# Two edits to a hand-ordered graph kernel: the order of its four long neighbour lists, and ScalarE's queue in the order of the plan

## The chip, the core and the metric

The kernel runs on one core of a Trainium2 chip. Its engines are TensorE (PE in the profile, with its weight loads as PEld), VectorE (DVE), ScalarE (ACT), GpSimd (POOL) and SyncE (SP), which here only issues DMAs. The metric is the device time of one execution in microseconds; the median over several executions is given.

## What is computed

The input is 16 graphs (`b`) of 1024 nodes with 64 channels, a dense weighted adjacency matrix per graph (mean degree of a few, a few nodes with dozens of neighbours) and a node mask that is all ones. Two layers follow each other:

```python
# layer 0
h = relu(layernorm(x))
x = x + (adj / max(adj.sum(2), 1)) @ h
# layer 1
h = relu(layernorm(x))
# nb[i]: neighbours of i without i.  A node with more than 10 of them
# drops every ceil(m/2)-th one; a pair dropped by either end is gone.
adj_d = dilate(adj, mask)
agg = 0.25*q(0.25) + 0.5*q(0.5) + 0.25*q(0.75)   # per channel, over h of the
                                                 # neighbours left and the node itself,
                                                 # quantiles interpolated between two values
y = relu((h + agg) @ W1 + b1) @ W2 + b2
x = x + y * mask
```

The quantiles need the neighbours' values in sorted order, for each of 64 channels. That sorting, on lists of very different length, is what most of the kernel is about.

## The kernel before

**Two stages.** In the first, the batch stage (0 to about 895 us in the trace), the 16 graphs go through one after the other. Each has eight tiles of 128 adjacency rows. ScalarE takes the sign of a tile (`sg<-at`), VectorE multiplies it with column keys and takes the largest eight keys of each of four segments (`rec<-sg`): these are the neighbour numbers. TensorE transposes the same tile (`pt<-ident,at`), ScalarE copies it out of PSUM (`att<-pt`), and TensorE multiplies it with h (`ps_small<-att,h`). The layer norms are on ScalarE and VectorE. Each node's record is scattered by GpSimd to a DRAM table (`srt<-row`) in order of degree, within groups of four graphs, and its normalised channels are written to a table `tab` per group.

**Jobs.** When a group of four graphs is complete, its nodes are worked off as jobs of `T` times 128 nodes with lists of equal length `n`, longest first. A job has the same parts always (class `Job`, L831): GpSimd gathers the neighbours' rows, one indirect DMA per list position (`places<-tab,idx`); VectorE opens the job (`rem`, `gone`, `ok`, `valid`, `q`, `wu`); ScalarE adds a huge number to the places that are gone (`places<-places,gone`); VectorE runs a sorting network of min and max operations between `places` and `other`; VectorE makes the weights (`w`) and ScalarE or VectorE the weighted values (`prod<-places,w`); TensorE adds these up (`pt<-ident,prod`) and runs the two small matrix products, with ScalarE copies between (`ot`, `hid`); VectorE adds the residual (`y`), and GpSimd scatters the rows to the output (`out_dram<-y`).

**Long lists.** The eight nodes of highest degree in each graph make the first long list, the next eight the second, and so on: four lists of 128 nodes with up to 88, 31, 24 and 20 neighbours (`LONG`, L43; `long_lists`, L1239). They gather from `whole`, a table of all graphs, so they can only run after the last graph. For each list, GpSimd fetches the 128 full adjacency rows (`lat`), VectorE picks the neighbours out of them (`lkey`, `lfound`, `lkeys`) down to indices (`lidx`), and a job follows, whose tiles carry an l (`lplaces`, `lgone`, `lw`). The 88 list has a gather buffer of its own (`lplaces0`); the other three share two (`lplaces`). All four share one second sorting buffer, `long_other` (L945): a list's network can start only after TensorE has read the products of the list before it out of that buffer. In a long list ScalarE writes the weighted values in place, into `lplaces` and `long_other`. The second stage, from about 895 us, holds the jobs that are left of the third group, all of the last group's, and the four long lists.

**What sets the order.** `Plan` (L234) records every instruction through a wrapper (hence the one line L228 in all rows). The work is cut into streams that yield an engine and an earliest time at each point; `Plan.run` (L323) always takes the stream that can begin first by the plan's own clocks, which `note` (L271) advances with a time per operation. An instruction is emitted when its stream is taken. The engines named in `manual_schedule` (L365) execute in this order of emission; the queues of the others are ordered by the framework's scheduler. In the kernel before, VectorE and GpSimd are named. ScalarE's, TensorE's and SyncE's queues are the scheduler's, and ScalarE's departs from the order of emission at 251 points of its queue. The order is static in either case.

Ranks break ties in the plan: `-600 + l` is a long job's gather rank and `100 * NG + l` its sorting rank, where `l` numbers the lists.

Of the kernel before, what the change touches and what calls it, by code (L numbers as in the profile page):

```python
# [39 lines left out]
LONG = (88, 31, 24, 20)  # L40
# [179 lines left out]
class Timed:  # L220


    def __init__(self, plan, name, engine):
        self._plan, self._name, self._engine = plan, name, engine
# [9 lines left out]
class Plan:  # L234
# [4 lines left out]
    def __init__(self, nc):  # L239
        names = {"vector": "DVE", "scalar": "ACT", "tensor": "PE", "gpsimd": "POOL", "sync": "SP"}  # L240
        self.nc = SimpleNamespace(
            **{attr: Timed(self, name, getattr(nc, attr)) for attr, name in names.items()}
        )
        self.clock = dict.fromkeys([*names.values(), "DMA"], 0.0)
        self.ready, self.used, self.users = {}, {}, {}
        self.slots, self.streams = {}, []
        self.last = self.own = None
        self.parts = set()

    def tile(self, pool, shape, dtype, name, bufs, users=0):  # L250

        res = pool.tile(shape, dtype, name=name, bufs=bufs)
        self.slots.setdefault(name, []).append(res.tensor.name)
        self.users[res.tensor.name] = users
        return res
# [12 lines left out]
    def at(self, *tiles):  # L268
        return max(self.ready.get(t.tensor.name, INF) for t in tiles)

    def note(self, engine, op, args, kwargs):  # L271
        if self.own is not None:
            self.clock[engine] = max(self.clock[engine], self.own)
        out = kwargs["out"] if "out" in kwargs else args[0]
        rest = [*args[0 if "out" in kwargs else 1:], *(v for k, v in kwargs.items() if k != "out")]
        rest = [getattr(v, "ap", v) if type(v).__name__.startswith("Indirect") else v for v in rest]
        rest = [v for v in rest if isinstance(v, bass.AP)]
        size = max(math.prod(v.shape[1:]) for v in (out, *rest[:2]))
        start = max(
            self.clock[engine],  # L280
            *(self.ready.get(v.tensor.name, 0.0) for v in rest if self.own is None),
            self.used.get(out.tensor.name, 0.0) if self.own is None else 0.0,
        )
        after = 0.15
        apart = engine == "SP" and out.tensor.name in self.parts
        if apart:
            start = max(self.clock[engine], *(self.ready[v.tensor.name] for v in rest))
        if engine == "DVE":
            half = op == "tensor_tensor" and all(v.dtype == HF for v in (out, *rest))
            time = 0.04 if op == "memset" else 0.07 + size * (0.57e-3 if half else 1.04e-3)  # L290
        elif engine == "ACT":
            pointers = sum(isinstance(kwargs.get(k), bass.AP) for k in ("bias", "scale"))
            time = 0.06 + size * 0.86e-3 + 0.11 * pointers + 0.09 * ("accum_out" in kwargs)
        elif engine == "PE":
            time = 0.1 + math.prod(out.shape[1:]) * 0.88e-3
            if op == "matmul" and rest[0].dtype == F32:
                time *= 2
        elif engine == "POOL":
            time, after = (1.27, 2.2) if op == "indirect_dma_start" else (0.15, 0.1)
            self.last = None  # L300
        else:
            start = max(start, self.clock["DMA"])
            busy = math.prod(out.shape) * 4 / 165e3

            time, after = 0.05, 2.2 + busy * (1 if 4 * out.shape[-1] >= 512 else 2)
            self.clock["DMA"] = start + busy
        self.clock[engine] = end = start + time
        if not apart:
            self.ready[out.tensor.name] = end + after
        for v in rest:  # L310
            self.used[v.tensor.name] = max(self.used.get(v.tensor.name, 0.0), end + after)
        if "accum_out" in kwargs:
            self.ready[kwargs["accum_out"].tensor.name] = end + after
        return start
# [21 lines left out]
@with_exitstack  # L336
def kernel(
    ctx: ExitStack,
    tc: tile.TileContext,
    x: bass.AP,  # L340
    adj: bass.AP,
    nodemask: bass.AP,
    w1: bass.AP,
    b1: bass.AP,
    w2: bass.AP,
    b2: bass.AP,
    out: bass.AP,
):

    nc = tc.nc
    B = x.shape[0]  # L360

    flags = ctx.enter_context(tc.tile_pool(name="flags", bufs=1))
    go = flags.tile([P, 1], I32, name="go")

    with tc.manual_schedule(engines={mybir.EngineType.DVE, mybir.EngineType.Pool}):  # L365
        list_path(tc, x, adj, nodemask, w1, b1, w2, b2, out, go)
    taken = nc.values_load(go[0:1, 0:1], min_val=0, max_val=1)
    with tc.If(taken > 0):
        with tc.For_i(0, B, 1) as b:
            dense_path(tc, b, x, adj, nodemask, w1, b1, w2, b2, out)  # L370
# [3 lines left out]
def list_path(ctx, tc, x, adj, nodemask, w1, b1, w2, b2, out, go):  # L374
# [7 lines left out]
    NG = len(GROUPS)  # L382
# [101 lines left out]
    whole = dram.tile([B * TS, W], F32, name="whole")  # L484
# [11 lines left out]
    plan = Plan(nc)  # L496
    plan.parts.update(tab.tensor.name for tab in tabs)
    nc = plan.nc
    new, free, room, at = plan.tile, plan.release, plan.room, plan.at
# [739 lines left out]
    def long_lists(pool):  # L1239
# [1 line left out]
        yield "DVE", always  # L1241
        rev = new(pool, [P, N], HF, "rev", 1)
        nc.vector.tensor_scalar(rev, col_f, -1.0, float(N), op0=OP.mult, op1=OP.add)
        for l, K in enumerate(LONG):
            n = K + 1
            yield "SP", always
            S = new(pool, [P, 1, RW], F32, "lS", 4)
# [62 lines left out]
            for e in range(2):  # L1310
# [7 lines left out]
            yield "DVE", lambda: 0.0 if progress["groups"] == NG else INF  # L1318
            job = Job(
                pool, n, 1, keys, idx.unsqueeze(1), node, mask, nodes_i, whole, S, NG,  # L1320
                *(("lplaces", 2) if l else ("lplaces0", 1)), -600 + l, begin=at(whole),
            )
            plan.add(job.run(), 100 * NG + l)

    progress = {"batches": 0, "begun": 0, "groups": 0, "ahead": 0, "jobs": [0] * (NG + 1)}
    for g in range(NG - 1):
# [1 line left out]
    with tc.tile_pool(name="lay0", bufs=2) as pool:  # L1328

        for stream, first in (  # L1330
            (endings, 0), (channels, 1), (products, 2), (transposes, 4), (listing, 5),
            (beginnings, 6), (loads, 7), (signs, -15),
        ):
            now = [0]
            plan.add(stream(pool, now), lambda first=first, now=now: 10 * now[0] + first)
        plan.run(lambda: progress["batches"] == B)
    with tc.tile_pool(name="long", bufs=1) as pool:

        plan.add(group(NG - 1, pool, "last_"), -2000)
        plan.add(long_lists(pool), -1500)  # L1340
        plan.run()
# [292 lines left out]
```

## Time and profile before

| what | before |
|---|---|
| median of 3 executions | 1513.86 us (1511.95 to 1516.6) |
| the profiled execution, whole | 1512.82 us |
| its span, first to last instruction | 1511.0 us |
| VectorE busy, 0 to 900 us | 81% |
| GpSimd busy, 900 to 1300 us | 75% |
| indirect DMAs issued by GpSimd after 900 us | 407 |
| one gather on GpSimd: busy, and start to start | 0.94 us, 1.25 us |
| first and last gather of the 88 list | 953.8 us, 1093.9 us |
| its opening, its weights (`lrem`, `lw` on VectorE) | 1096.5 us, 1346.8 us |
| networks of the 31, 24 and 20 lists begin | 1394.4, 1436.0, 1470.5 us |
| last scatter to the output begins | 1502.1 us |

A row of the groups reads: line, engine, operation, the tile written and those read, shape, number of instructions; then busy time and mean duration; then the time the engine idled just before, and what ended it. A row of the waits reads: who waited, for whom, total in us, how many times, the longest.

### The profile page before, as it was taken

How to read it: one execution, taken by the hardware profiler on the slowest of the kernel's cores; microseconds unless marked ns; L12 is line 12 of the kernel's file. 1: busy time of each engine (PE TensorE's matmuls, PEld its weight loads, DVE VectorE, ACT ScalarE, POOL GpSimd, SP SyncE). 2: the span in 40 equal slices, each digit the busy share in tenths (PEclk: the TensorE clock that was granted, in tenths of full speed). 3: DMA queues.
4: the chain of work that ended last, by engine and by line, in shares of the span. 5: the costliest groups of instructions: out<-in, count | busy, mean ns of one | idle time of the engine just before them, and what ended most of it. 6: DMA issues, size and time to landing. Idle time of an engine off the chain costs nothing. (4 is left out here: it accounts for less than half of the span.)

```text
span 1511.0 us, 15983 instructions
## 1 busy us (share of the span) xinstructions
PE 738.8 (49%) x3192; PEld 464.7 (31%) x3192; DVE 1191.3 (79%) x4104; ACT 816.4 (54%) x2789; POOL 957.2 (63%) x1154
## 2 busy tenths in 40 slices
PE   4778777327877556567667620024000123228542
PEld 2434334214544233343444320012000122216432
DVE  6777798997899779859869869893059999986875
ACT  7989878557879457757975520201050223148341
POOL 0122227777678757757777787667777777765083
PEclk8889888658888777869688755555555565558765
DMA  5445665424355253355341242111111111211010
GB/s 177 150 142 168 163 210 160 123 73 114 101 162 152 59 174 94 99 126 161 94 140 31 60 101 68 50 37 28 30 26 23 28 28 40 44 33 22 2 25 13
DMA packets 135718, 133.36 MB, mean 88 GB/s; under 512 B 100756, under 2 KB 103444, under 8 KB 135492
## 3 DMA queue, kind: packets, MB, share of 16 engines
q1 hardware_dynamic: 102876, 90.79, 20.8%
q0 software_dynamic: 32736, 41.47, 11.2%
q14 instruction: 78, 0.64, 0.1%
q8 instruction: 28, 0.46, 0.1%
HBM read 112.90 MB, written 23.61 MB: 90 GB/s over the span
## 5 line engine op out<-in xcount | busy, mean ns | idle before, releaser
L228 POOL DMA_INDIRECT places<-tab,idx x372 | 370.2, 995 | 131.7 <-issue 101.8
L228 PE MATMUL pt<-ident,prod 128*128 128x128 f32 (+1 forms) x736 | 160.2, 377 | 517.8 <-DVE prod L228 241.2
L228 PEld LDWEIGHTS pt<-ident,prod 128*128 128x128 f32 (+1 forms) x736 | 129.3, 256 | 550.4 <-ACT prod L228 412.4
L228 PE MATMUL ps_small<-att,h 128*65 128x512 f32 x512 | 254.7, 644 | 27.3 <-ACT h L228 10.5
L228 POOL DMA_INDIRECT srt<-row,to x128 | 125.9, 984 | 165.8 <-ACT row L228 144.0
L228 PE MATMUL pt<-ident,at 128*128 128x128 f32 x1024 | 176.7, 320 | 96.0 <-ACT att L228 71.1
L228 POOL DMA_INDIRECT lplaces<-whole,lidx x163 | 167.2, 1026 | 55.6 <-issue 48.5
L228 DVE MAX8 rec<-sg 128x8 f16<-128x256 f16 x512 | 180.1, 414 | 4.4
L228 PEld LDWEIGHTS pt<-ident,at 128*128 128x128 f32 x1024 | 136.9, 164 | 143.5 <-ACT att L228 93.8
L228 ACT ACTIVATE sg<-at 128x1024 f16<-128x1024 f32 x128 | 134.8, 1054 | 75.0 <-DMA at<-in_adj_dram 65.7
L228 ACT COPY att<-pt 128x512 f32<-128x512 f32 x256 | 141.9, 582 | 20.7 <-PE pt L228 18.8
L228 POOL DMA_INDIRECT places<-tab,last_idx x124 | 123.8, 998 | 41.3 <-issue 35.0
L228 PEld LDWEIGHTS ps_small<-att,h 128*65 128x65 f32 x512 | 74.7, 151 | 161.9 <-issue 123.2
L228 ACT ACTIVATE places<-places,gone 128x64 f32<-128x64 f32 x496 | 123.5, 335 | 0.5
L228 ACT ACTIVATE prod<-places,w 128x64 f32<-128x64 f32 x213 | 54.1, 336 | 120.5 <-DVE w L228 120.5
L228 POOL DMA_INDIRECT out_dram<-y,nodes_i x93 | 91.8, 987 | 22.6 <-issue 15.1
L228 DVE TENSOR_TENSOR sg<-sg,keyed 128x1024 f16<-128x1024 f16 x128 | 87.2, 681 | 23.7 <-ACT sg L228 23.7
L228 ACT ACTIVATE gone<-gone 128x15 f32<-128x15 f32 (+9 forms) x40 | 8.2, 206 | 169.2 <-DVE ok L228 169.0
L228 DVE TENSOR_TENSOR long_other<-lplaces 128x512 f32<-128x512 f32 (+5 forms) x124 | 64.1, 555 | 29.1 <-ACT lplaces L228 28.9
L228 DVE TENSOR_TENSOR other<-places,other 128x64 f32<-128x64 f32 (+6 forms) x204 | 69.6, 341 | 5.9
L228 PE MATMUL ps_small<-ot,w_sb 128*128 128x128 f32 (+3 forms) x112 | 47.6, 513 | 44.2 <-DVE y L228 31.2
L228 DVE TENSOR_TENSOR places<-places,other 128x64 f32<-128x64 f32 (+2 forms) x208 | 62.3, 309 | 4.9
(231 smaller groups left out, 1670.8 us busy)
## 6 DMA issues: line engine op xcount, KB each, us to landing
at<-in_adj_dram SPq DMA_DIRECT2D x128, 512.0 KB
places<-tab,idx POOLq DMA_INDIRECT x372, 2.5
whole<-tab SPq DMA_DIRECT2D x4, 1057.0 KB
tab<-row SPq DMA_DIRECT2D x16, 264.0 KB
xt<-in_x_dram SPq DMA_DIRECT2D x16, 256.0 KB
lplaces<-whole,lidx POOLq DMA_INDIRECT x163, 2.4
srt<-row,to POOLq DMA_INDIRECT x128, 2.7
places<-tab,last_idx POOLq DMA_INDIRECT x124, 2.4
```

The source lines that it names most:

```text
L228: ins = getattr(self._engine, op)(*args, **kwargs)
```

## The change

Three things are edited. ScalarE joins the engines whose queue keeps the order of emission. The long lists are run in the order 31, 24, 88, 20, with ranks that follow this order; which rows a list holds, its buffers and its capacities stay with the list. And the plan's clock counts a TensorE instruction as 1.5 times as long from the end of the batch stage on.

```diff
@@ class Plan, __init__
         self.parts = set()
+        self.pace = 1.0
@@ class Plan, note, TensorE
             time = 0.1 + math.prod(out.shape[1:]) * 0.88e-3
             if op == "matmul" and rest[0].dtype == F32:
                 time *= 2
+            time *= self.pace
@@ tile_gnn_kernel
-    with tc.manual_schedule(engines={mybir.EngineType.DVE, mybir.EngineType.Pool}):
+    with tc.manual_schedule(engines={mybir.EngineType.DVE, mybir.EngineType.Pool, mybir.EngineType.Activation}):
@@ long_lists
-        for l, K in enumerate(LONG):
+        for nth, l in enumerate((1, 2, 0, 3)):
+            K = LONG[l]
@@ long_lists
-                *(("lplaces", 2) if l else ("lplaces0", 1)), -600 + l, begin=at(whole),
+                *(("lplaces", 2) if l else ("lplaces0", 1)), -600 + nth, begin=at(whole),
             )
-            plan.add(job.run(), 100 * NG + l)
+            plan.add(job.run(), 100 * NG + nth)
@@ list_path, after the batch stage
         plan.run(lambda: progress["batches"] == B)
+    plan.pace = 1.5
     with tc.tile_pool(name="long", bufs=1) as pool:
```

No instruction's kind or shape changes but for a few of ScalarE's and VectorE's products, which the plan shares between the two by its clocks (2405 instructions on ScalarE before, 2431 after; 4025 and 4023 on VectorE; 1154 and 1152 on GpSimd; 296 on SyncE in both). VectorE's and GpSimd's queues are the same as before up to the first list's `lkey` operations, 918.9 us in the trace before; ScalarE's, TensorE's and SyncE's differ from the start.

## The prediction

> **What bounds the kernel now.** I read the page first, then the engines' waits, then the timeline of the last 600 us by engine, then the chain that ended last.
>
> ```profile
> span 1511.0 us, 15983 instructions
> PE 738.8 (49%) x3192; PEld 464.7 (31%) x3192; DVE 1191.3 (79%) x4104; ACT 816.4 (54%) x2789; POOL 957.2 (63%) x1154
> DVE  6777798997899779859869869893059999986875
> ACT  7989878557879457757975520201050223148341
> POOL 0122227777678757757777787667777777765083
> DVE lrem L228 <- DMA lplaces<-whole,lidx: 50.1, 2, 48.9
> DVE y L228 <- PE ps_small L228: 28.1, 4, 14.1
> DVE sg L228 <- ACT sg L228: 23.7, 15, 8.7
> DVE other L228 <- ACT places L228: 14.2, 7, 4.8
> ...
> 1096.53 0.34 DVE L228 TENSOR_TENSOR lrem<-lplaces,lS 128x176 f32<-128x176 f32 x1 [48.89 <-DMA lplaces<-whole,lidx]
> 1378.07 0.57 DVE L228 TENSOR_TENSOR other<-places 128x384 f32<-128x384 f32 x1 [11.20 <-ACT places L228]
> 1394.38 1.22 DVE L228 TENSOR_TENSOR long_other<-lplaces 128x512 f32<-128x512 f32 x2
> 1425.18 0.20 DVE lw L228
> 1425.40 0.35 ACT long_other L228
> 1491.27 3.93 ACT L228 ACTIVATE lplaces<-lplaces,lw 128x64 f32<-128x64 f32 x16 [18.76 <-DVE lw L228]
> 1502.09 0.96 POOL L228 DMA_INDIRECT out_dram<-y,lnodes_i  x1 [1.73 <-DVE bad L1346]
> ```
>
> VectorE is the bound: busy in nearly every slice but those of the digits 3 and 0 (about 1020 to 1096 us), where it waits 14.1 us for a `y` and 48.9 us for the 88 list's gathers. ScalarE is at 8 to 9 tenths only in the first 200 us. From 900 us GpSimd gathers without a pause, 1.25 us apart, to 1382 us. The end is a chain of VectorE, ScalarE and TensorE through the lists 31, 24 and 20, one after the other, because all share `long_other`.
>
> **What the Trainium skill says.** PSUM — Partial Sum Buffer, Engine vs sequencer instructions: "ScalarE/VectorE/GpSimdE queues are strict FIFO." So the order of a queue is a cost by itself: the trace agrees, ScalarE sat 51.7 us before `lgone` until 1097.47. DMA: Bandwidth & Descriptors, Anatomy of one DMA, gives about 2 us fixed per DMA; here a gather lands 2.4 us after its issue. TensorE: Matmul & The Clock Gate, What's actually happening: an idle array runs at half clock; the page shows PEclk 5 from 900 to 1340 us.
>
> **Part 1, ScalarE's queue.** It adds and removes nothing; it takes 251 departures out of the queue (the order of instructions shows none left, so the edit does what it says). Up to the end of the batch stage the kinds that move most are the 128 `row<-rec` (36.1 us in all), 16 `row<-row_f` and 26 `prod<-S`: fillers that ran up to 170 us early and that nobody but a late scatter waits for. Without them, `att<-pt` goes back 7 places in the mean and the work that VectorE waits for (places, prod, norms) forward 3 to 4. VectorE's waits for ScalarE in this stage are 23.7 (sg) + 14.2 (places) + 17.5 (ln_v, two rows) = 55.4 us: the most that could be gained. What could be lost: behind a ScalarE instruction that waits stand `att` copies, then TensorE's two `pt` buffers, then the `at` buffers and SyncE's loads. In the places where an instruction's producer ended later in the trace before than something now behind it, the exposure of the real work is 3 to 13 us at some forty places, on an engine with 30% slack from 200 us on; in the first 200 us ScalarE idles 24 us, which fillers used. SyncE's and TensorE's queues are re-ordered with it, by the scheduler. Bounds: -35 to +20 us; I take 0, since VectorE's own order is unchanged and the swaps are a few places.
>
> **Part 2, the lists, up to the 88 list's opening.** The order of instructions gives GpSimd from 943 us: 31 + 24 + 88 gathers, 1 of list 20, 2 `lat`, 4 `places`, 6 scatters = 156 x 1.25 = 195 us, plus waits for indices. VectorE builds a list's indices in about 20 us (957.1 to 977.0 for 31; 34 for 88), and GpSimd's next `lat` needs the build before it: estimated from these lengths 4.6 us for list 88's `lat` (indices of list 24 ready at 965, GpSimd free at 960.6), 9.3 us for list 20's (ready at 1007, free at 997.5) and 3.5 us for list 31's `y`, which stands in GpSimd's queue among the 88 gathers. SyncE's four loads per list (`lS`, 891 to 901 us) change places among themselves only, before anything needs them. Sum: last gather issued 943 + 195 + 17 - 1 = 1154, opening at about 1156 instead of 1096.5. VectorE meanwhile does more: before 180 us from 916.3, of which 63 idle, so 117 us of work; now also the networks 31 (1394.4 to 1425.0: 30.6) and 24 (1436.0 to 1461.1: 25.1), 173 us in 240. Idle 67 instead of 63: **the wait isn't removed, the 88 list just comes 60 us later with 56 us more done.**
>
> **Part 3, from there to the 88 list's weights.** Before: 1096.5 to 1346.8 = 250.3 us, with 17 us at its start when ScalarE marks 88 places (21.1 us). Now the jobs are further ahead: VectorE did 28.6 us of job work between 1346.8 and 1394.4 (47.6 less waits of 5, 11, 2 and 1); of that kind only 11.7 us are left after `lw` in the new order. So 17 us move ahead of it: 1156 + 250 + 17 = 1423. GpSimd's gathers for these jobs are all in by then (264 us of its queue after 1156, scatters that wait included, ends before VectorE needs them), so it isn't the limit.
>
> **Part 4, the handover of `long_other`.** Before, `lw` at 1346.8, ScalarE's 67 products of the 88 list among job work until 1379.7, TensorE's sums until 1392, next network at 1394.4: 47.6 us, which VectorE filled with 28.6 us of jobs. VectorE's network 20 needs two things: list 20's marks by ScalarE, and TensorE done with `long_other`. Now `lw` at 1423; in ScalarE's queue between there and list 20's marks stand 67 products of list 88, 31 of two jobs with their two copies, 17 marks of the last two jobs, and 6 small ones, 123 at 0.245 us (24 took 5.82 us), and five of 0.6 us (`ot`, `hid`): 33 us, 1457; 20 marks 5 us; TensorE's last 58 products stand behind a `hid` at 1460 and take 13 to 16 us (before: 122 records in 13.5 us). Network 20 begins at 1474 (50 us after `lw`), with 12 us of cover. It takes 20.4 us as before (1470.5 to 1490.9): `lw` of list 20 at 1494.5.
>
> **Part 5, the end.** Before, 20 us from that `lw` (1490.9) to the end, one scatter after the last `y`. Now ScalarE's `ot` copies for two jobs stand behind list 20's 16 products (3.9 us), their sums behind 17 matmuls of list 20 in TensorE's queue (6 us), so `y` of the 88 list comes about 14 us after `lw`, and 13 scatters follow one another from there: 13 x 1.27 = 16.5. Last scatter begins at lw + 29, and 8.9 us follow it (1502.1 to 1511.0): 37 us. Span 1494.5 + 37 = 1531.5.
>
> **Part 6, pace.** It moves no instruction by itself in the batch stage (set after it); what it does to the order is in the counts above.
>
> Sum: span +20.5 us; the profiled execution is 1.8 us longer than its span and 1.0 below the median shown. Forecast 1512.82 + 20.5 = **1533 us**, 1.3% above the median.
>
> **Rivals.**
> A (faster): ScalarE in VectorE's order ends VectorE's waits. For: its rows of waits, 55.4 us in the batch stage, and 11.2 us at 1378 behind the 88 list's products. Against: ScalarE's departures were mostly fillers. At two thirds of 55.4, -37: 1496. It decides from 24 us on.
> B (faster): the handover is hidden better: TensorE adds up as ScalarE writes, as for list 31 (products 1425.7 to 1431.5, sums to 1434.2), network 20 at 1460 and the end 12 us shorter: 1533 - 26 = 1507. Against: 58 of 67 sums stand behind the late `hid`.
> C (no effect): old and new idle match and the scatters at the end overlap: 1514.
> D (slower still): ScalarE, ahead of VectorE, blocks `att` copies and starves the loads: +20 in the batch stage, 1553. For: SyncE waited 323.8 us for TensorE to free `at`. Against: four signs are kept ahead.
>
> **How the numbers follow.** Main case 0.48 (own range 1518 to 1546), A 0.19, B 0.08, C 0.10, D 0.15. Faster by over 0.3% (about what a measurement of this kernel can tell from no change) 0.27, within 0.10, slower 0.63. Range 1498 to 1552: half of A and of D are left out.
>
> **What would show it.** Right: `lrem` of 88 places near 1156 with a wait of some 30 us before it; `lw` of 67 near 1423; a VectorE gap of about 35 us before network 20; a row of scatters after the last `y`. Part 1 shows in the time of `last_recs` work (896 us before). Wrong: that time moved by over 15 us, no gap before network 20, or the 88 list's opening before 1140.

## The result, and the profile after

| | before | after |
|---|---|---|
| median | 1512.9 us (1508.1 to 1516.6, 4 runs) | 1593.0 us (1592.7 to 1601.1, 4 runs) |
| span of the profiled execution | 1511.0 us | 1590.6 us |
| first stage: start to the first work on `last_recs` | 901.4 us | 971.5 us |
| second stage: from there to the end | 609.6 us | 619.1 us |

The change makes the kernel slower by 5.3% (ratio 1.0532, 95% interval 1.0506 to 1.0558). The forecast, 1533 us, had the direction and missed the size. Of the 79.6 us of span, 70.1 are lost before the first long list is touched, and 9.5 after. (From here on a stage is measured from the first `last_keys<-last_recs` on VectorE. The expectations of e1 to e4 count from VectorE's first instruction on `last_recs`, which comes 5 us earlier: 896 us before, 966 after.)

The first fence is from the page of the changed kernel: the span, the engines' busy times, and the slices of VectorE, ScalarE and GpSimd.

```profile
span 1590.6 us, 15958 instructions
PE 789.8 (50%) x3192; PEld 495.9 (31%) x3192; DVE 1193.0 (75%) x4102; ACT 826.0 (52%) x2815; POOL 960.3 (60%) x1152
...
DVE  7666698996687778778749878799750699999851
ACT  7788877656676736574876450114310423221651
POOL 0122227777557763776776487767777877377614
```

VectorE has the work it had (1193.0 us, before 1191.3), but where the slices of the first stage had eights and nines there are sixes, sevens and eights. Nothing was added: the same work waits more. The table of waits of the changed kernel (who waited, for whom; total us, times, longest) says for what:

```profile
DVE sg L228 <- ACT sg L228: 81.0, 40, 8.7
DVE lrem L228 <- DMA lplaces<-whole,lidx: 45.0, 2, 44.4
DVE long_other L228 <- ACT lplaces L228: 37.0, 9, 12.0
DVE y L228 <- PE ps_small L228: 32.1, 6, 11.8
DVE deg L228 <- PE ps_small L228: 30.6, 8, 7.4
...
ACT sg L228 <- DMA at<-in_adj_dram: 94.5, 37, 14.6
...
PE pt L228 <- ACT att L228: 162.2, 59, 8.9
...
SPq L228 <- PE pt L228: 390.5, 110, 15.6
```

Before, VectorE's rows were 23.7 us for `sg` by ScalarE and 50.1 for the 88 list's gathers, and the last three were these:

```profile
ACT sg L228 <- DMA at<-in_adj_dram: 65.7, 27, 24.5
...
PE pt L228 <- ACT att L228: 74.4, 45, 7.4
...
SPq L228 <- PE pt L228: 323.8, 102, 15.8
```

So the 88 list's wait, which the new list order moves, is nearly all still there. What grew is a chain through four engines: TensorE waits 88 us more for ScalarE's `att` copies, SyncE 67 us more for TensorE, ScalarE 29 us more for loads, VectorE 57 us more for signs.

The rows don't add up to the loss, because other waits of TensorE got shorter: in the first stage it waited 17 us for the jobs' products (`prod`) instead of 102. Taken whole, the same 2432 matmul records of TensorE's first stage were busy for 615.0 us instead of 588.8, and TensorE stood idle for 356.5 us instead of 312.7. So 44 of the 70 us are more standing still, and 26 are the same work taking longer.

One stretch of the changed kernel's timeline shows how this goes (start and duration in us, engine, operation, and in brackets the idle time before it and what ended it):

```profile
555.06 1.05 ACT L228 COPY att<-pt 128x512 f32<-128x512 f32 x2
...
555.68 1.97 PE L228 MATMUL pt<-ident,at 128*128 128x128 f32 x8 [0.22 <-ACT att L228]
...
565.45 0.37 SPq L228 DMA_DIRECT2D y<-srt  x1
...
565.92 0.41 SPq L228 DMA_DIRECT2D at<-in_adj_dram  x1
...
570.73 1.06 ACT L228 ACTIVATE sg<-at 128x1024 f16<-128x1024 f32 x1 [14.62 <-DMA at<-in_adj_dram]
...
571.78 0.46 ACT L228 ACTIVATE hid<-ps_small,b_sb 128x256 f32<-128x256 f32 x1
...
572.14 1.06 ACT L228 COPY att<-pt 128x512 f32<-128x512 f32 x2
...
572.29 0.79 PE L228 MATMUL ps_small<-b_sb,ones_f 1*128 1x128 f32 x2 [14.64 <-ACT hid L228]
```

TensorE finished eight transposes (both `pt` buffers) at 557.7. Their two copies could have run then. They stand in ScalarE's queue behind an `sg` whose load SyncE issued only at 565.9, and ScalarE stands still for 14.6 us in front of it. TensorE stands still just as long, for the `hid` behind the same `sg`. The load itself was late here for a reason outside this chain: its buffer had been free since 556.8, when TensorE's last transpose out of it ended, but in SyncE's queue it stood behind a job's load (`y<-srt`), which the profile shows waiting for GpSimd's scatters to the output, 11.7 us. So the stretch shows what a late load does to the copies, not that the copies made this load late. Such hold-ups of SyncE are not what grew: over the stage a buffer lay free for 0.9 us in the mean before its next load was issued, and for 0.6 us in the changed kernel.

Of all time in which ScalarE stood still while a finished `pt` waited for its copy, 153 us fell to an `sg` in the changed kernel, 26 us before (worked out from the trace: gaps of over 0.3 us between the end of the fourth transpose and the start of its copy, by the instruction after the gap).

Two of the five sets of runs below (e5, x4, x5, x6 and z2, z3) fell into spells in which the kernel before itself took 1978 and 1956 us, so their times are given only as ratios to it, and since x4, x5 and x6 gave other ratios when they were run again (as y4, y5 and y6), these ratios settle little.

### The profile page after: what moved, and what is told of

The parts are those of the page before. It is cut to its first block, busy times and chain, and to the rows that moved or that the text cites. A ratio compares the mean times of both kernels' runs of the same rounds, so it can differ in the third digit from the quotient of the medians.

```text
span 1590.6 us, 15958 instructions
## 1 busy us (share of the span) xinstructions
PE 789.8 (50%) x3192; PEld 495.9 (31%) x3192; DVE 1193.0 (75%) x4102; ACT 826.0 (52%) x2815; POOL 960.3 (60%) x1152
## 5 line engine op out<-in xcount | busy, mean ns | idle before, releaser
L228 POOL DMA_INDIRECT places<-tab,idx x372 | 374.5, 1007 | 162.9 <-issue 102.7
L228 PE MATMUL ps_small<-att,h 128*65 128x512 f32 x512 | 270.3, 677 | 17.0 <-DVE row L228 7.0
L228 PE MATMUL pt<-ident,at 128*128 128x128 f32 x1024 | 190.1, 340 | 162.2 <-ACT att L228 139.4
L228 PEld LDWEIGHTS pt<-ident,at 128*128 128x128 f32 x1024 | 147.9, 174 | 214.9 <-ACT att L228 165.4
L228 POOL DMA_INDIRECT lplaces<-whole,lidx x163 | 162.7, 998 | 49.7 <-issue 48.1
L228 POOL DMA_INDIRECT places<-tab,last_idx x124 | 127.5, 1029 | 57.2 <-issue 35.3
L228 PEld LDWEIGHTS ps_small<-att,h 128*65 128x65 f32 x512 | 78.6, 159 | 159.2 <-issue 133.3
L228 ACT ACTIVATE prod<-places,w 128x64 f32<-128x64 f32 x239 | 60.3, 335 | 93.4 <-DVE w L228 93.3
L228 DVE TENSOR_TENSOR long_other<-lplaces 128x512 f32<-128x512 f32 (+6 forms) x124 | 64.0, 555 | 37.2 <-ACT lplaces L228 37.0
L228 PE MATMUL ps_small<-ot,w_sb 128*128 128x128 f32 (+3 forms) x112 | 51.7, 553 | 48.4 <-ACT ot L228 46.3
L228 ACT COPY ot<-pt 128x128 f32<-128x128 f32 (+3 forms) x56 | 21.9, 392 | 95.4 <-PE pt L228 95.2
```

The lines of the kernel that those rows point to most:

```text
L228: ins = getattr(self._engine, op)(*args, **kwargs)
```

## The experiments

The theory H: the loss is ScalarE's queue in the first stage. An `att` copy that stands in line keeps a `pt` buffer, TensorE keeps the `at` buffer, SyncE's next load starts later. The rivals: the lists' edit carries the loss (L); TensorE's and SyncE's queues do, which the scheduler re-orders when ScalarE's is fixed (S); ScalarE merely stands idle behind late operands (W); the plan's TensorE clock is at fault (K).

**1. The change taken apart.** Four kernels, each with a part of the change.

e1_act: the kernel before with

```diff
-    with tc.manual_schedule(engines={mybir.EngineType.DVE, mybir.EngineType.Pool}):
+    with tc.manual_schedule(engines={mybir.EngineType.DVE, mybir.EngineType.Pool, mybir.EngineType.Activation}):
```

> ScalarE's queue in the order of the plan, alone; lists in the old order, no pace. Theory H (the loss sits in ScalarE's queue in the batch stage: att copies, which the scheduler let pass other work, wait in line, TensorE's two pt buffers and SyncE's loads follow): last_recs work at 966 us as in the changed kernel, not 896, and then the old second stage of about 595 us: 1580 us (1565 to 1600). Rival L (the lists' edit carries the loss, through TensorE's and SyncE's queues, which the scheduler orders over the whole kernel): 1513 to 1545 us.

e2_lists: the changed kernel with that line as before.

> The lists' order and the pace, without ScalarE. H: last_recs work at 896 us within 5, then a second stage of 604 to 615 us as in the changed kernel or as my prediction's parts 2 to 5 have it: 1523 us (1510 to 1535). L: last_recs work late by tens of us, 1550 or more.

e3_act_first: the kernel before, its schedule cut in two where the batch stage ends, ScalarE named in the first part only. The edit at the seam:

```diff
         plan.run(lambda: progress["batches"] == B)
+    manual.__exit__(None, None, None)
+    manual = tc.manual_schedule(engines={mybir.EngineType.DVE, mybir.EngineType.Pool})
+    manual.__enter__()
```

> ScalarE in the order of the plan in the batch stage only, lists and pace as before. H: all of the loss of this stage, last_recs work at 966 us, then 595 us: 1583 us, and not below the run with ScalarE in both stages by more than 10 us. If ScalarE's order in the second stage has a price of its own, this one is faster than that run by it.

e4_lists_act_second: the changed kernel cut in the same way, ScalarE named in the second part only.

> The whole change, but ScalarE's queue left to the scheduler in the batch stage. H: last_recs work at 896 us, then the changed kernel's 604 us: 1522 us (1512 to 1535). L: 1560 or more.

The stages are those of the profiled execution.

| | time | ratio (95%) | first stage | second stage |
|---|---|---|---|---|
| before | 1515.7 | | 901.4 | 609.6 |
| e1: ScalarE, both stages | 1604.7 | 1.057 (1.0538 to 1.0602) | 973.2 | 631.5 |
| e3: ScalarE, first stage | 1589.0 | 1.0476 (1.0443 to 1.051) | 976.1 | 609.7 |
| e2: lists and pace | 1520.4 | 1.0031 (1.002 to 1.0043) | 900.9 | 614.9 |
| e4: lists, pace, ScalarE second | 1531.9 | 1.0098 (1.0072 to 1.0123) | 909.7 | 621.8 |
| the whole change | 1593.0 | 1.0532 | 971.5 | 619.1 |

L falls: with the lists alone the first stage is as before. Each first stage with ScalarE in plan order is 70 to 75 us longer. The lists cost 5.3 us in the second stage. ScalarE's order costs 22 us there with the old lists (e1 against e3), but only 4.2 with the new ones (the whole change against e2): the new order of the lists suits a fixed ScalarE queue better, and that half of the edit repairs part of the other. e2 came 3 us below its 1523. e1 came 5 us above its range and e3 16 us below e1, where at most 10 were expected: the price of ScalarE's order in the second stage was not in H's sum. e4 was expected at 1522 and came 10 us later, still within its range. Its first stage is 9 us longer than e2's; 4 of them are there before the seam, where the two kernels run the same queues, so that much is the difference of one execution from another.

**2. ScalarE's queue alone.** Fixing one queue lets the scheduler re-order the others, so e1 doesn't yet say whose queue it is. Two kernels fix TensorE's and SyncE's queues as well; between them only ScalarE's differs, the other four queues being instruction for instruction the same. m1 is the kernel before with the edit below; m2 names ScalarE's engine (Activation) in the same set as well.

```diff
-    with tc.manual_schedule(engines={mybir.EngineType.DVE, mybir.EngineType.Pool}):
+    with tc.manual_schedule(engines={mybir.EngineType.DVE, mybir.EngineType.Pool, mybir.EngineType.PE, mybir.EngineType.SP}):
```

> The kernel before, with TensorE's and SyncE's queues in the order of the plan too, ScalarE's left to the scheduler. A base for the next run. Theory H (ScalarE's place in line): ScalarE's queue still lets att copies pass, so last_recs work stays within 15 us of 901 and the time within 1500 to 1535 us. Rival S (part of the 70 us comes from TensorE's and SyncE's queues, which the scheduler re-orders when ScalarE is fixed): this alone moves the time by 25 us or more, to 1540 or beyond.

> As the run before, with ScalarE's queue in the order of the plan as well: VectorE's, GpSimd's, TensorE's and SyncE's queues are instruction for instruction those of that run, only ScalarE's differs. H: last_recs work 60 us or more later than there, att copies start 3 us after their transposes instead of 1.5; the time 75 to 100 us above that run, as ScalarE alone cost 89 us. S: under 45 us above it.

m1 took 1529.3 us (1.0087, 1.0057 to 1.0117), m2 1592.8 (1.0518, 1.0485 to 1.055). ScalarE's queue alone is worth 63.5 us: 40 in the first stage (916.5 to 956.7) and 21 in the second. That is under the 75 to 100 that H expected, and above S's 45; H's first stage was to grow by 60 or more, and the copies to start 3 us after their transposes, where m2 has 2.4 (m1 1.4). So ScalarE's queue is the main cause, not quite the only one: fixing TensorE's and SyncE's cost 15 us of the first stage, and in e1, where the scheduler ordered them around the fixed ScalarE, the first stage is 16 us longer than in m2. TensorE's and SyncE's waits in m1, then in m2:

```profile
PE pt L228 <- ACT att L228: 61.5, 57, 6.4
...
SPq L228 <- PE pt L228: 409.2, 94, 26.2
```

```profile
PE pt L228 <- ACT att L228: 179.7, 75, 9.2
...
SPq L228 <- PE pt L228: 524.3, 108, 28.1
```

With TensorE's queue untouched it waits 118 us more for the copies, and SyncE 115 us more for TensorE. The links of the chain follow from ScalarE's order. In sum TensorE stands idle 27 us longer in the first stage and is busy 13 us longer.

**3. The copies' place in line.** In the changed kernel a copy starts 3.0 us after the fourth of its transposes has ended, in the mean of all 256, before 1.5 us: 387 us more in sum. In 216 of these ScalarE is busy, for the most part with other work (77 with `sg`, 36 with marks of places, 34 with products, 18 with `row<-rec`), in 171 it stands still. (The first expectation below has 257 and 131; these count ScalarE instructions that overlap twice.) The plan gives a copy the rank 10 b + 3 for graph b, and jobs of the first group have 0 to 9, so where both could begin a copy goes last. Two kernels give the copies the first rank, with ScalarE's queue fixed (x1) and left to the scheduler (x2).

```diff
-                    plan.add(turned(st, hf, k, h2, pt), 10 * b + 3)
+                    plan.add(turned(st, hf, k, h2, pt), -1000)
```

> The changed kernel, but an att copy takes the first rank in the plan (-1000 instead of 10 b + 3), so that it is emitted ahead of other ScalarE work that could begin at the same time. H: what the copies waited behind was mostly other ScalarE work placed ahead of them (257 of the 387 us that they wait more), so the wait falls to 1.5 us or less in the mean, last_recs work comes back to 900 to 925 us, and the time to 1520 to 1550. Rival W (the cost is ScalarE standing idle behind instructions whose operands are late, 131 us of the 387, which no rank removes): last_recs work at 950 or later, 1570 or more.

> The same rank, ScalarE's queue left to the scheduler: VectorE's and GpSimd's queues are those of the run with the rank, so the difference between the two is ScalarE's queue alone, the new plan's effect on VectorE taken out. H: close to the run with the lists' edit alone, 1505 to 1530 us, and 10 to 30 us under the run with the rank. W: 55 us or more under it.

x1 took 1558.7 us (1.0279, 1.0251 to 1.0306), first stage 928.8; x2 1529.9 (1.0097, 1.0067 to 1.0126), first stage 902.0. The wait of a copy fell to 1.86 us, not to 1.5. x1 came out 9 us above H's range, 11 below W's: 43 of the 70 us go with the rank, and 27 us stay against x2, all in the first stage (the second stages, 628.2 and 626.7, are alike, and 12 us longer than e2's). They aren't ScalarE's queue alone, as the second expectation has it: TensorE's and SyncE's queues, which the scheduler orders around it, differ between x1 and x2 too, from 13 us on. TensorE's row in x1 is almost that of before:

```profile
PE pt L228 <- ACT att L228: 83.0, 73, 6.3
```

TensorE's busy and idle time in the first stage (us) says where the 27 us lie:

| | matmul records | busy | idle | first stage |
|---|---|---|---|---|
| before | 2432 | 588.8 | 312.7 | 901.4 |
| changed | 2432 | 615.0 | 356.5 | 971.5 |
| m1 | 2432 | 599.8 | 316.7 | 916.5 |
| m2 | 2432 | 612.7 | 344.0 | 956.7 |
| x1 | 2396 | 617.1 | 311.7 | 928.8 |
| x2 | 2396 | 587.4 | 314.6 | 902.0 |

With the rank TensorE stands idle no longer than before. What is left between x1 and x2 is the same number of matmuls taking 30 us more. So the copies' place in line is the larger half; the rest shows as slower work on TensorE, of which the last section has more. No run changed that speed by itself, so that it causes the 27 us is not shown.

**4. What the other half is.** Theory G: a ring of `sg`, copies, buffers and loads, closed by an `sg` that the plan gives out before its load has landed. x5 is the changed kernel with the first of these edits, x6 has the first rank as well, and x4, K's test, has the second edit alone.

```diff
-                    at(st["rows"][t]) if t in st["rows"] else INF, room("sg", 4),
+                    at(st["rows"][t]) + 4.0 if t in st["rows"] else INF, room("sg", 4),
```

```diff
-        self.pace = 1.0
+        self.pace = 1.5
```

> The changed kernel, but the plan gives out a sign of a tile (sg) 4 us later than its load lands by the plan's clock. Theory G (a ring: in ScalarE's queue an sg waits for its load and holds the att copies behind it, these hold TensorE's pt buffers, TensorE's transposes hold the at buffers, and those hold SyncE's next loads, for which the next sg waits; in the changed kernel 153 us of standing in front of att copies that were due fell to an sg, 26 before): that figure falls below 80, last_recs work comes to 920 to 950 us instead of 971, the time to 1540 to 1572. Rival N (an sg given out later only comes later, VectorE gets it later by as much): 1585 us or more.

> Both the first rank for the att copies and the later sg. G: the two add up, last_recs work at 905 to 922 us, 1525 to 1545 us. N: no better than the rank alone, 1555 or more.

> The changed kernel with the pace of 1.5 for TensorE from the start on, not from the end of the batch stage. Theory K (the order of the plan is bad for ScalarE because the plan's TensorE is too fast there, so that copies are given out before they can run): last_recs work at 945 us or earlier, 1565 or less. G: the loads' times in the plan stay as they are, last_recs work at 955 to 985, 1575 to 1605.

These three took 1.0484 (1.0443 to 1.0526), 1.0345 (1.0302 to 1.0387) and 1.1047 (1.1007 to 1.1087) times the kernel before beside them. They were run again:

> The changed kernel with every sg given out 4 us later than its load lands by the plan's clock, once more, on another chip: on the first one every kernel, the one before too, took 30% longer. Theory G (the ring of sg, att copies, pt and at buffers, loads): the time in which an sg waits in front of att copies that are due falls from 153 us to below 80, last_recs work comes to 920 to 950 us, the time to 1540 to 1572. Rival N (it only comes later): 1585 or more.

> First rank for the att copies and the later sg, once more. G: both add up, last_recs work at 905 to 922 us, 1525 to 1545 us. N: no better than the rank alone, 1555 or more.

> The changed kernel with TensorE's pace of 1.5 from the start on, once more. Theory K (ScalarE's order is bad because the plan's TensorE is too fast in the batch stage): 1565 us or less. G: loads and signs stay where they are, and the ring turns no faster: 1575 or more; the ratio of 1.105 on the slow chip speaks for more than that, up to 1670.

| | time | ratio (95%) | first stage | standing before `sg` while a copy is due | TensorE waits for copies |
|---|---|---|---|---|---|
| before | 1514.3 | | 901.4 | 26 | 74.4 |
| changed | 1593.0 | 1.0532 | 971.5 | 153 | 162.2 |
| y5: `sg` 4 us later | 1605.8 | 1.0604 (1.0575 to 1.0634) | 999.6 | 198 | 185.0 |
| y6: and first rank | 1602.3 | 1.0573 (1.0546 to 1.06) | 973.8 | 86 | 119.8 |
| y4: pace 1.5 throughout | 1792.7 | 1.1832 (1.1802 to 1.1862) | 1184.5 | 298 | 235.3 |

G's and K's numbers fell; N's came true in both runs, and y4 is above every range. As a remedy G is out: with a later `sg` ScalarE stands longer before it (198 us instead of 153). As a remedy K is out too: the slower TensorE costs another 213 us of first stage. But y4 didn't bring the plan nearer to the chip. By the formula in `note` the plan's TensorE needs about 684 us for the first stage before (an estimate: the formula times the trace's counts), where the trace has 588.8 us busy; at 1.5 that is 1026 us, more than the stage of 901.4 us. A transpose alone is off the other way, 0.21 us in the plan and 0.32 in the trace. A plan with each kind of instruction at its measured time was not run. An `at` buffer is given back in the plan only when both its `sg` and its transposes have been given out, so pushing either back pushes the next load back, and the ring grows. This account of why is argued, not shown. y4's rows are the changed kernel's, larger:

```profile
ACT sg L228 <- DMA at<-in_adj_dram: 219.1, 71, 8.9
...
SPq L228 <- PE pt L228: 537.0, 102, 25.0
```

**5. Who holds the buffer.** For each of the 128 tiles the traces give when SyncE issues its load, when ScalarE's `sg` runs, when the eight transposes start and end, and when the next load into the same buffer is issued (means, us):

| | load to `sg` | load to first transpose | the eight transposes | load to next load | first stage |
|---|---|---|---|---|---|
| before | 9.5 | 26.3 | 4.1 | 31.2 | 901.4 |
| e2 | 9.4 | 26.3 | 4.1 | 31.2 | 900.9 |
| m1 | 8.4 | 26.9 | 4.0 | 31.7 | 916.5 |
| x1 | 10.9 | 28.4 | 3.5 | 32.5 | 928.8 |
| m2 | 7.6 | 29.1 | 4.2 | 33.3 | 956.7 |
| changed | 7.7 | 28.9 | 4.6 | 34.0 | 971.5 |
| y5 | 8.3 | 29.8 | 4.3 | 35.3 | 999.6 |
| y4 | 6.4 | 36.5 | 5.9 | 42.6 | 1184.5 |

Five buffers and 128 tiles make 25.6 rounds, and 25.6 x (34.02 - 31.18) = 73 us, the loss. This sum is near to an identity, since loads fill the stage. What isn't an identity is who holds the buffer last: before and after, TensorE is the last to need the buffer in 98 of 100 tiles, 20 to 25 us after the sign. So TensorE's transposes, not the busiest engine, say when the next load starts, and VectorE follows with its `sg`. That this sets the pace of the whole stage is read from these columns and from m1 and m2. Two kernels were to test it at the buffers: three `pt` and two `ps_small` in the changed kernel (z3), and six `at` with four `y` in the kernel with the lists alone (z2); the first and the second pair of lines here, with the counts in the pools and in the plan to match.

```diff
-        pt = new(ps_t, [P, HALF], F32, "pt", 2, users=1)
+        pt = new(ps_t, [P, HALF], F32, "pt", 3, users=1)
@@ the other kernel
-                st["rows"][t] = new(pool, [P, N], F32, "at", 5, users=2)
+                st["rows"][t] = new(pool, [P, N], F32, "at", 6, users=2)
```

> The changed kernel with three pt buffers instead of two and two ps_small instead of three, in the plan as well. Theory T (the batch stage runs at the pace at which an at buffer comes free, which TensorE's transposes decide in 98 of 100 tiles; in the changed kernel the transposes of one tile take 4.56 us instead of 4.08 because TensorE waits 162 us instead of 74 for att copies): with a third pt buffer a late copy no longer stops TensorE, its waits for att copies fall below 100 us, issue to issue of the same at buffer from 34.0 to 32.5 us or less, last_recs work to 935 or earlier, 1530 to 1560 us. Rival Q (TensorE's own order, its transposes start late whatever the copies do): 33.5 us or more, 1580 or more.

> The lists' edit and the pace, ScalarE left to the scheduler, with six at buffers instead of five (four y instead of six make the room). If the ring of at buffers limits the batch stage by its length (a tile holds its buffer for 31.2 us, five of them), a sixth makes the loads up to 6/5 as fast until VectorE's 81% are full: last_recs work at 850 to 885 us, 1475 to 1508. If TensorE's rate limits (then each buffer is just held longer, some 37 us): 1512 to 1530.

As ratios to the kernel before, z3 came to 1.0634 (1.0602 to 1.0665) and z2 to 1.0233 (1.0203 to 1.0263). Neither gains anything. With z3 the price of the `ps_small` given up can't be told from the worth of the `pt`, nor with z2 that of the two `y`, behind whose loads SyncE's next `at` can stand. z2 leans to TensorE's rate and against the ring's length: with six buffers a tile holds its own for 51.7 us, with five in e5 (below; the same first stage but for these buffers, and 1991 us in all against 2000) for 41.6. Both stay inconclusive.

**6. The second stage.** e5 takes the pace away from e2:

```diff
-    plan.pace = 1.5
```

> The order of the lists alone, no pace, ScalarE left to the scheduler. With pace the two cost 5 us. If the pace, which moves no instruction of the batch stage, only shifts the choices of the second stage, this is within 8 us of it, 1512 to 1529; if it carries the lists' order (my prediction counted on it in part 6 only through the counts), 1535 or more.

The ratio is 1.0069 (1.0053 to 1.0085), e2's 1.0031. This leans against a pace that carries the lists' order; it doesn't settle it, since other ratios of that set didn't repeat. x8 gives the 88 list a second sorting buffer of its own, on the base of e2:

```diff
+            apart = "long_other0" if self.name == "lplaces0" else "long_other"
@@
-                room("other" if short else "long_other", 1),
+                room("other" if short else apart, 1),
@@
-                other = Bt = new(pool, [P, n, T, C], F32, "long_other", 1, users=1)
+                other = Bt = new(pool, [P, n, T, C], F32, apart, 1, users=1)
```

> The lists' edit and the pace, ScalarE left to the scheduler, and a long_other of its own for the 88 list, so that the network of the 20 list needn't wait until TensorE has read the 88 list's products. My part 4 (the handover of long_other is what makes VectorE wait between lw of 67 weights and network 20; 10.8 and 6.4 us of gaps there with the lists alone): network 20 begins within 25 us of that lw instead of 36.4, and the time falls by 8 to 18 us against 1520, to 1502 to 1512. Rival: VectorE has no other work left there, and the wait moves to the 88 list's y and the scatters at the end: 1515 to 1525.

1521.0 us (1.0046, 1.0033 to 1.0059), e2's 1520.4: no gain. Network 20 begins 36.6 us after `lw` of 67 weights, with one buffer (e2) 36.7. Its line in x8's timeline names what it waits for:

```profile
1427.81 0.22 DVE L228 TENSOR_TENSOR lw<-lwu 128x67 f32<-128x67 f32 x1
...
1464.43 0.83 DVE L228 TENSOR_TENSOR long_other<-lplaces 128x512 f32<-128x512 f32 x2 [14.39 <-ACT lplaces L228]
```

Not the buffer: list 20's own marks, which ScalarE makes after the 88 list's 67 products. The rival named the right outcome for another reason; the wait didn't move to the `y`, it was never the buffer's.

No kernel tried was faster than the one before.

## Why the prediction was wrong, step by step

**The direction.** The forecast's whole +20.5 us lay in the second stage, which grew by 9.5. That the time moved the way it said is for the most part luck: it came from a term that the forecast put at 0.

**The bound.** "VectorE is the bound" read busy shares. It is the busiest engine, but in the first stage its inputs came at the pace of the loads, and TensorE's transposes, last to need each buffer, released the loads. The row that said so, SyncE's 323.8 us behind TensorE, was quoted only as a point for rival D. VectorE isn't out of this chain: of TensorE's 312.7 us of idle time in that stage 102 went to jobs' products that VectorE and ScalarE make, and no run tells what that is worth. And ScalarE is not at 8 to 9 tenths in the first 200 us alone: its row has 8 or 9 again in the slices at about 230, 380, 450 and 720 us.

**Part 1, ScalarE's queue: taken 0, bounds -35 to +20; measured +70.** This is the step that failed. Three arguments stood in it. That VectorE's order is unchanged: true, and no protection, since its inputs came later. That the swaps are a few places (a copy 7 places back in the mean): true, but 256 copies, each 1.5 us later, are 387 us of lateness. And that ScalarE has 30% slack: the slack didn't help a copy that stood in line, because TensorE has two `pt` buffers and stopped for it. The prediction's own "3 to 13 us at some forty places" are 120 to 520 us in all, and this slack is what set them at nothing. TensorE waited 88 us more for copies, stood idle 44 us more in sum and worked 26 us longer, and the stage became 70 us longer. With TensorE's and SyncE's queues held the same, ScalarE's order alone cost 40 us of first stage and 21 of the second (m1, m2). The gain side was read well as far as it went: the signs do run sooner after their load (7.7 us instead of 9.5), but the loads are later.

**Rival D** had the mechanism word for word (`att` copies blocked, loads starved) and a price of 20 us, of which nothing in the profile was the source. Pricing it per copy, as the page allowed, would have widened the bound: 7 places at ScalarE's mean of 0.293 us (816.4 / 2789), times 256 copies, is an estimate of 525 us of lateness, set against two `pt` buffers; 387 were measured. Its counter-argument, four signs ahead, doesn't bear on it: the buffer isn't held by signs.

**Part 2, the 88 list's opening: right.** Predicted 1156, which is 255 us after the stage begins (at 901.4 in the trace before); measured 256.5 (256.6 in e2). Idle until then 67 us predicted, 67 measured (7.2 + 7.4 + 8.4 + 44.4). The wait isn't removed, as the prediction said.

**Part 3, its weights: right.** Predicted 267 us later, that is 522; measured 524.0.

**Part 4, the handover: too long by 14 us.** Predicted 50 us from `lw` to network 20, measured 36.4. The timeline of the changed kernel:

```profile
1495.42 0.22 DVE L228 TENSOR_TENSOR lw<-lwu 128x67 f32<-128x67 f32 x1
...
1499.52 0.34 ACT L228 ACTIVATE long_other<-long_other,lw 128x64 f32<-128x64 f32 x1
...
1528.35 0.43 PE L228 MATMUL pt<-ident,long_other 128*64 128x128 f32 x2
...
1528.61 3.92 ACT L228 ACTIVATE lplaces<-lplaces,lgone 128x64 f32<-128x64 f32 x16
...
1531.05 12.88 PE L228 MATMUL pt<-ident,lplaces 128*64 128x128 f32 x116
1531.85 0.83 DVE L228 TENSOR_TENSOR long_other<-lplaces 128x512 f32<-128x512 f32 x2 [11.98 <-ACT lplaces L228]
```

The 58 last sums do stand behind a late `hid` and do take 12.9 us, as predicted; but they read `lplaces`. Of the 67 products one lies in `long_other`, and TensorE has read it by 1528.8. The network waits for ScalarE's marks and begins as the last of them are written; these end 37.1 us after `lw`, where the prediction had 39. VectorE's gap before it is 12.0 us, with 7.9 before a `y` ahead of it, where the prediction looked for one of about 35. So the count of ScalarE's queue was right, and the second need of the network, TensorE's sums, wasn't one. The row `ACT long_other x1` beside `ACT lplaces` would have told it. x8 agrees. Rival B had network 20 at 1460 on the time scale of before; measured, it begins 560.4 us after the stage does, 1461.8 on that scale. B's shorter end didn't come.

**Part 5, the end: right.** Predicted 20.4 us of network and 37 us of tail; measured 20.3 and 38.4.

**Sum.** Second stage predicted +20.5 us, measured +9.5: part 4's 14 too many, and 3 too few in parts 2, 3 and 5. First stage predicted 0, measured +70.1. The second alone would have given 1522 us, within the range; the first is the whole miss.

**Part 6, the pace,** moves nothing in the first stage when set after it, as said: the changed kernel and e1, which has no pace, run the same ScalarE and TensorE queues through it. Rivals A and C are out: VectorE's waits for ScalarE grew, and the time moved.

**What stays open.** Why TensorE's work takes 30 us longer in x1 than in x2, and whether that is the cause of the 27 us of first stage between them or comes with it. The chain of copies, buffers and loads is seen in the traces and follows from ScalarE's order (m1, m2), but no run took the late `sg` or the buffers away alone with success.

## What to carry to other kernels

Before fixing the order of a queue, find which buffer sets the pace of the stage and who gives it back last; then price every instruction that hands such a buffer on by its lateness, not by its engine's busy share. Here an order made from a plan's clocks cost 63.5 us on the engine whose short copies free another engine's two buffers; the scheduler's order, in which these copies started 1.5 us after their transposes, was worth keeping. A row of waits that grows isn't yet a loss: set it against the busy and idle time of its engine. When a network or sum waits for a buffer, count which of its operands really lie in it.

## What the hardware showed that was not expected

The same TensorE work got longer when it was spread out: 3192 matmul records took 738.8 us busy before and 789.8 after, with the mean granted clock at 0.699 and 0.675. A transpose of a tile's block took 320 ns in the mean before and 340 after, a product with `att` 644 and 677. The rows of the pages, before and after:

```profile
L228 PE MATMUL pt<-ident,at 128*128 128x128 f32 x1024 | 176.7, 320 | 96.0 <-ACT att L228 71.1
...
L228 PE MATMUL pt<-ident,at 128*128 128x128 f32 x1024 | 190.1, 340 | 162.2 <-ACT att L228 139.4
```

The means hide two speeds: most transposes take about 272 or about 421 ns. Those over 350 ns are 27% before and 41% after, and they lie behind stops of TensorE. In the changed kernel 79% of the transposes that begin within 4 us of the end of a stop of over 1 us are slow, and none of the 397 that begin 8 us or more after it (before: 73%, and 8 of 553). The first stage has 59 such stops before and 93 after. So part of a wait comes back as slower work on the engine that waited.
